# A masked-adjacency kernel: engine order remade for the loads' landing marks, a second bank for the counts, finer last loads, and two late drains on VectorE

## The chip, the cores and the metric

One core of a Trainium2 chip runs the kernel. The metric is the device time of one execution in microseconds (us). Before the change it is 188.82 us, the median of three runs (188.42 to 188.97).

## What is computed

```python
h = relu(layernorm(x))                    # x: 4096 x 64, fp32
support = h @ weight                      # 64 x 64
mask = adj != 0                           # adj: 4096 x 4096, fp32 (64 MB)
rank = cumsum(mask, axis=1); deg = rank[:, -1:]
k = minimum(deg, 100); pos = rank - (deg - k)
w = mask * where(pos > 0, 0.5 ** (k - pos), 0)
out = x + w @ support + bias
```

Each row of the adjacency keeps its last 100 neighbours and weights them by powers of one half, counted from the row's end. The output is small. The 64 MB of `adj` have to come in once.

## The kernel before

Rows are taken in 32 **tiles** of 128 rows. One tile is 2 MB of `adj` and takes this way:

- SyncE issues `load` (line 295) into one of NA = 4 buffers `a_sb`. Tiles 0, 1 and 28 to 31 come as two loads of four column groups, the others as one load of eight.
- VectorE runs `convert` (L496: nonzero test to bytes), one instruction for each load, and `flip` (L506: 32x32 block transposes into `mt`).
- TensorE runs `totals` (L512, 8 matmuls into a PSUM tile of pool `ps_t`). ScalarE runs `split` (L517), TensorE `suffix` (L526, 9 matmuls, again in `ps_t`), and VectorE `clamp` (L530). These count, for each block, the neighbours to its right.
- TensorE runs `place` (L538 and L542, 8 and 16 matmuls) into four PSUM tiles of pool `ps_v`, one for each j. ScalarE runs `weigh` (L551, Exp) four times, one j each, into a weight buffer `wk`.
- For each pair of tiles, TensorE runs `aggregate` (L559): 8 steps of 4 matmuls with `hr`, which holds `support` in two parts, into the PSUM tile `acc`.
- For each four tiles, `drain` (L572, ScalarE) takes `acc` out and adds the bias, `turn_back` (L580, TensorE) transposes back, `finish` (L586, VectorE) adds `x`, and a store follows. The last four tiles are drained in two halves.

Ahead of this stands a **prologue**: TensorE turns and centres `x`, ScalarE squares and rectifies it, VectorE takes the root, `scale` (L472) forms `support`, and `first` (L479, ScalarE) and `second` (L482, VectorE) write `hr`. The intermediate tensors lie in `early`, which is one of the NW = 2 weight buffers. Two weight buffers are all there are, so the `weigh` of tile 2 can start only when the four `second` no longer need `early`. GpSimd builds constants, among them the matrices `near`, `rest` and `far` of `order_of` (L375 to L389).

**What sets the order.** `tasks()` lists every step with its engine, an assumed duration, what it needs, and the pool that it takes a buffer from. `plan()` walks through it like a scheduler: on each engine it takes the step with the smallest due time from the table `DUE` among those that can start soon. The program is emitted in that order, and a dependency of each instruction on the one ahead of it on its engine keeps it there. So every engine works its list in order, and an instruction that waits holds all behind it. `plan()` assumes that a load has landed as soon as its bytes have been moved.

PSUM is given out as NV = 6 tiles of `ps_v`, NB = 1 of `ps_t`, and one `acc`. With NB = 1, `totals`, `suffix` and `turn_back` all take turns in one tile.

Of the kernel before, what the change touches and what calls it, by code (L numbers as in the profile page):

```python
# [8 lines left out]
F32 = mybir.dt.float32  # L9
# [22 lines left out]
STEP = {t: 4 for t in (0, 1, 28, 29, 30, 31)}  # L32
LOADS = [(t, h, h + STEP.get(t, 8)) for t in TILES for h in range(0, 8, STEP.get(t, 8))]

PARTLY = {31}
PARTED = (0, 1, 0, 2), (1, 2, 0, 1), (1, 2, 1, 2)
DRAINS = [(g, 0, 4, True) for g in range(7)] + [(7, 0, 2, True), (7, 2, 4, True)]
STORES = [(0, 0, 16), (1, 0, 12), (1, 12, 14), (1, 14, 16)]
NA, NM, NT, NW, NV, NB = 4, 4, 4, 2, 6, 1

DUE = {
    "fetch": [-1003, -1847],
    "load": [65, 1148, 1192, 1344, 890, 882, 1059, 807, 177, 1469, 585, 426, -306, 496, -49, 266, 921, 615, 495, 273,
    509, 817, 887, 432, 1250, 832, 1156, 645, 31, 863, 872, 512, 638, 869, 1362, 792, 926, 1009],
    "load_rest": [-481],
    "turn": [-213, 892, -361, 828, -409, -147, 168, -107],
    "turned": [-404, -273, 1152, 128, 503, 511, 433, -263],
    "center": [-857, -641, -1350, -827],
    "square": [139, -1681, -2148, -2029],
    "relu": [217, 890, -64, 143],  # L50
    "spread": [-1274, -1134, -743, -201],
    "support": [458, 166, -823, -732],
    "scale": [31, 1087, -17, 582],
    "root": [-38],
    "power": [-305],
    "constants": [-1199, 288],
    "order_of": [1110],
    "count": [174],
    "counted": [-242],
    "first": [1030, 859, 446, 134],  # L60
    "second": [869, 310, 488, 149],
    "convert": [799, 235, 213, 621, 871, 221, 1137, 339, 665, 170, 840, 839, 269, 846, 1322, 763, 1208, 992, 1053, 1092,
    755, 1566, 506, 1283, 1017, 914, 1881, 1297, 1713, 1456, 1930, 1878, 1817, 1254, 2527, 1603, 1404, 1849],
    "flip": [755, -234, 295, -127, 442, -299, 314, 236, -95, 42, 943, 437, 1189, 848, 1722, 445, 670, 663, 1043, 1071,
    1018, 1159, 1502, 907, 1558, 1730, 1512, 1723, 625, 1907, 1701, 1739, 1719, 1519, 1418, 1515, 1365, 795],
    "totals": [163, 587, 208, 187, -888, 339, 133, -152, 475, 1157, 159, 135, 674, 545, 1071, 817, 439, 1024, 1281,
    1461, 443, 2052, 963, 1181, 926, 1932, 1537, 584, 1513, 1671, 1316, 1615],
    "split": [-294, -174, -1849, -575, -454, -698, -618, -971, -742, -275, 300, 6, -214, 155, -90, -143, 509, 616, 114,
    395, 584, 524, 615, 13, 506, 320, 818, 391, 1992, 1302, 1105, 460],
    "suffix": [265, 470, 626, 553, 76, 351, -120, 701, -560, 193, 222, 311, 159, 444, 810, -221, 772, 1294, 1743, 886,  # L70
    718, 429, 591, 1159, 1296, 2185, 1511, 1501, 2001, 1496, 2127, 1546],
    "clamp": [-739, 475, 354, 317, -585, 294, 102, -276, 538, 118, 920, -398, 130, 1157, 352, 866, 900, 81, -363, 492,
    698, 1569, 702, 757, 515, 1132, 736, 1149, 1495, 1590, 1729, 1541],
    "place": [841, 96, 498, 879, 824, 837, 808, 522, 1103, 1914, 1312, 1548, 862, 1225, 743, 1302, 1785, 1644, 1994,
    1697, 1566, 1560, 1577, 1633, 2537, 1922, 1847, 2364, 2393, 2364, 1714, 1845],
    "weigh": [1655, 1181, 868, 631, 1236, 404, 1584, 1443, 897, 269, 877, 841, 328, 1501, 418, 1096, 1670, 1095, 1290,
    1045, 1295, 1247, 1314, 999, 672, 1559, 1035, 1631, 1070, 1779, 1431, 1276, 2029, 1311, 1734, 1852, 1556, 1640,
    1599, 1881, 1168, 1820, 1423, 545, 1375, 1271, 1659, 2299, 2395, 2281, 2155, 2139, 2062, 2491, 1666, 1651, 1902,
    1875, 1618, 2485, 1751, 1754, 2523, 1796, 2184, 2358, 1409, 2593, 2132, 1541, 1713, 2047, 1583, 1456, 1562, 2282,
    1641, 1846, 1727, 2021, 2924, 2344, 2590, 1925, 1978, 2498, 1946, 1761, 2622, 1817, 2190, 1884, 1953, 2032, 2057,  # L80
    2381, 2020, 2701, 1854, 2394, 2313, 2255, 1976, 2259, 1957, 2012, 1591, 2429, 2382, 2260, 2365, 3172, 2928, 2044,
    3150, 1958, 2643, 2675, 2150, 3338, 2587, 2729, 2343, 2953, 1990, 2517, 2778, 3358, 2745, 2645, 3479, 2076, 3183,
    2758, 2299, 2866],
    "aggregate": [254, 1326, 1623, 59, 522, 1349, 93, 1245, 247, 484, 1268, 1686, 2132, 1190, 2358, 448, 974, 1308,
    1356, 611, 856, 1518, 486, 1545, 1236, 918, 398, 1827, 1513, 1406, 1117, 1500, 1296, 1193, 452, 1811, 1260, 1164,
    1961, 1568, 1038, 1010, 1127, 1422, 1532, 1050, 1941, 1756, 685, 1493, 1977, 1124, 1719, 1240, 1199, 787, 2328,
    1076, 2631, 1964, 1500, 1168, 989, 1906, 1959, 931, 1528, 1194, 1746, 1676, 1766, 1637, 1602, 1588, 2104, 1990,
    1832, 1942, 1495, 1697, 1592, 2020, 1907, 2085, 1379, 1230, 1622, 2213, 2061, 2515, 2853, 1453, 2287, 1736, 1377,
    1679, 1972, 1745, 1669, 2617, 3235, 2571, 1770, 2567, 1656, 2752, 2666, 1678, 2311, 2453, 2712, 2395, 2976, 2826,
    2628, 2119, 2143, 2488, 2511, 1602, 2160, 1962, 2594, 2032, 2291, 2585, 1920, 2821],  # L90
    "drain": [82, 374, 29, 620, 400, 1392, 1843, 1544, 1599],
    "turn_back": [572, 1129, 645, 1544, 2558, 1512, 1987, 1280, 2435],
    "finish": [79, 927, -547, 514, 1225, 592, 1061, 2342, 2532],
    "store": [8458, 8834, 7981, 9977],
}
WAIT = 250, 60, 150, 60, 0
PE, DVE, ACT, POOL, SP = range(5)


def tasks():  # L100
# [12 lines left out]
    for n, (t, _, _) in enumerate(LOADS):  # L113
        task("load", (n,), SP, n, 0, 0, [("convert", m) for m in range(n) if LOADS[m][0] == t - NA])
    task("load_rest", (), SP, 4, 0, 0, [("load", 2)])
    for h in range(2):
        for t0 in range(0, 16, 4):
            task("turn", (h, t0), PE, 0, 430, 680, [("fetch", h)], ("v", ("turned", h, t0)))
            task("turned", (h, t0), ACT, 0, 480, 640, [("turn", h, t0)])
    for n in range(4):  # L120
        task("center", (n,), PE, 1, 860, 1060, [("turned", 1, 12)], ("v", ("relu", n)))
        task("square", (n,), ACT, 1, 480, 640, [("center", n)])
        task("relu", (n,), ACT, 2, 480, 640, [("square", n)])
    for n in range(4):
        task("spread", (n,), PE, 2, 850, 1050, [("square", n)])
    for n in range(4):
        task("support", (n,), PE, 15, 890, 1090, [("relu", n), ("power",)], ("v", ("scale", n)))
        task("scale", (n,), DVE, 10, 610, 730, [("support", n), ("power",)])
    task("root", (), DVE, 3, 480, 600, [("spread", 3)])
    task("power", (), DVE, 3, 1950, 2010, [("root",)])  # L130
    task("constants", (0,), DVE, 0, 530, 620, [])
    task("constants", (1,), POOL, 6, 4500, 4600, [("constants", 0)])
    task("order_of", (), POOL, 1, 3500, 3600, [("constants", 0)])
    task("count", (), PE, 14, 180, 360, [("order_of",)], ("v", ("counted",)))
    task("counted", (), DVE, 14, 160, 250, [("count",)])
    for i in (0, 2, 1, 3):
        task("first", (i,), ACT, 15, 520, 650, [("scale", i % 2 * 2 + 1), ("support", 3)])
        task("second", (i,), DVE, 15, 610, 740, [("first", i)])
    for n, (t, k0, k1) in enumerate(LOADS):
        k = k1 - k0  # L140
        task("convert", (n,), DVE, when[t], 311 * k + 20, 311 * k + 190, [("load", n)], ("b", ("flip", n)))
        task("flip", (n,), DVE, when[t] + 2, 136 * k + 66, 136 * k + 186, [("convert", n)] + ([("place", t - NT)] if t >= NT else []))
    for t in TILES:
        due = when[t] + 3
        parts = range(len(PARTED)) if t in PARTLY else (0,)
        task("totals", (t,), PE, due, 330, 550, [("flip", n) for n, load in enumerate(LOADS) if load[0] == t], ("t", ("split", t)))
        task("split", (t,), ACT, due + 0.5, 476, 616, [("totals", t)] + ([("suffix", t - 2)] if t > 1 else []))
        task("suffix", (t,), PE, due + 1, 618, 838, [("split", t)], ("t", ("clamp", t)))
        task("clamp", (t,), DVE, due + 1.5, 391, 511, [("suffix", t), ("counted",)] + ([("place", t - 2)] if t > 1 else []))
        task("place", (t,), PE, due + 2, 700, 920, [("clamp", t), ("constants", 1)], ("v", *[("weigh", t, j, parts[-1]) for j in range(4)]))  # L150
        for part in parts:
            a0, a1, s0, s1 = PARTED[part] if t in PARTLY else (0, 2, 0, 2)
            hold = (a1 - a0) * (s1 - s0) * 213 + 52
# [3 lines left out]
    for u in range(16):  # L157
        t = 2 * u + 1
        for k in range(8):
# [3 lines left out]
            if k == u % 2 == 0 and u:  # L163
                needs.append(("drain", u // 2 - 1))
# [470 lines left out]
```

## Time and profile before

| | us |
|---|---|
| median of 3 runs | 188.82 |
| profiled execution | 188.37 |
| its span, first to last instruction | 186.7 |
| TensorE busy (2080 matmuls) | 164.9 |
| ScalarE busy | 152.1 |
| VectorE busy | 146.8 |
| GpSimd busy | 18.9 |
| DMA queue of the loads, share of 16 engines' span | 88.4% |

The page has, for each engine, busy time in 40 slices of 4.67 us; a chain of the work that ended last; and groups of equal instructions with their mean duration, the idle time ahead of them and what ended it. The timeline view lists instructions in order of time. Of each load the trace also records when each of its 16 parts landed; the last of these is called the load's **last mark** here. For tile 2 it comes at 22.1 us, for tile 3 at 27.0, then about every 4.9 us: tile 26 at 141.48, tile 27 at 146.39, the halves of tiles 28 to 31 at 148.92, 151.38, 153.87, 156.36, 158.85, 161.34, 163.83 and 166.32. Of the last load the first part landed at 162.88. In the text, tile numbers stand in brackets: `weigh`(30, 2) is j = 2 of tile 30, `aggregate`(14, 4) is step 4 of the pair of tiles 28 and 29.

### The profile page before, as it was taken

To read this page: it belongs to the slowest core of one execution; us is meant where nothing else is said; L and a number is where in the kernel's file an instruction comes from. 1 tells how busy PE (TensorE), PEld (TensorE's weight loads), DVE (VectorE), ACT (ScalarE), POOL (GpSimd) and SP (SyncE) were. 2 spreads that over 40 slices of the span, in tenths; PEclk is the share of its full clock that TensorE was granted. 3 is DMA by queue.
4 is the path that set the end of the run, shared out by engine and by line. 5 is a ranking of instruction groups with operands and counts; after the bars stand their busy time and mean duration, and the time that the engine had idled before them with its cause. 6 is when DMAs were issued, how large, how long until landed. Compare 5 with 4: busy or idle time off the path is not lost.

```text
span 186.7 us, 4747 instructions
## 1 busy us (share of the span) xinstructions
PE 164.9 (88%) x2080; PEld 127.3 (68%) x2080; DVE 146.8 (79%) x152; ACT 152.1 (82%) x198; POOL 18.9 (10%) x57
## 2 busy tenths in 40 slices
PE   7999699647989899889998997999898979897982
PEld 5957367435857768667676775877775858685881
DVE  3187499999999997799797899879798989993100
ACT  2773176912999999699999999999969799999951
POOL 7899500000000000000000000000000000000000
PEclk9997569999999999999999999999999999999999
DMA  6999999999999999999999999999999999940020
GB/s 202 390 427 435 435 420 425 416 428 428 428 414 428 434 414 432 428 414 442 411 428 428 418 432 421 418 446 411 428 421 414 413 420 416 417 201 0 12 90 16
DMA packets 6597, 69.55 MB, mean 373 GB/s; under 512 B 944, under 2 KB 1200, under 8 KB 1712
## 3 DMA queue, kind: packets, MB, share of 16 engines
q1 hardware_dynamic: 6416, 69.21, 88.4%
q8 instruction: 16, 0.26, 0.6%
q10 hardware_dynamic: 160, 0.03, 0.1%
q14 instruction: 5, 0.04, 0.1%
HBM read 68.19 MB, written 1.05 MB: 371 GB/s over the span
## 4 chain that ended last, share of the span: by engine, by line
ACT 36%; PE 32%; DVE 15%; POOL 10%; issue 5%; POOLq 0%; ACTq 0%
ACT wk L551 29%; PE acc L559 19%; DVE m L496 7%; ACT sums L517 5%; PE ps L526 5%; PE po L580 3%; DVE mt L506 3%; PE v L542 2%; DVE behind L530 2%; PE v L538 2%; PE tot L512 2%; ACT acc_sb L572 1%; DVE wk L472 1%; DVE hr L482 1%; POOL where L414 1%
## 5 line engine op out<-in xcount | busy, mean ns | idle before, releaser
L551 ACT ACTIVATE wk<-v 128x1024 fp32r<-128x1024 uint8 (+2 forms) x136 | 123.2, 1028 | 2.3 <-PE v L542 2.1
L496 DVE TENSOR_SCALAR m<-a_sb 128x4096 uint8<-128x4096 f32 (+1 forms) x38 | 84.8, 2238 | 5.0 <-DMA a_sb<-in_adj_dram 5.0
L559 PE MATMUL acc<-wk,hr 128*128 128x256 f32 x512 | 74.6, 291 | 3.7 <-ACT wk L551 2.2
L559 PEld LDWEIGHTS acc<-wk,hr 128*128 128x128 f32 x512 | 64.0, 188 | 10.6 <-ACT wk L551 4.3
L506 DVE STREAM_TRANSPOSE mt<-m 128x1024 f32<-128x1024 f32 (+1 forms) x38 | 40.7, 1072 | 0.4
L517 ACT ACTIVATE sums<-tot 128x512 f16<-128x512 uint8 x32 | 20.3, 634 | 16.4 <-PE tot L512 16.4
L530 DVE TENSOR_SCALAR behind<-ps,excess 128x256 f16<-128x256 f32 x32 | 15.4, 481 | 14.1 <-PE ps L526 13.9
L526 PEld LDWEIGHTS <-far 128*128 128x128 f16 x224 | 17.9, 101 | 1.9 <-POOL far L389 1.0
L526 PE MATMUL ps<-sums,far 128*128 128x224 f16 (+6 forms) x224 | 18.5, 225 | 0.7 <-POOL far L389 0.7
L512 PE MATMUL tot<-mt,band 128*32 128x256 f16 x256 | 13.5, 288 | 5.3 <-DVE mt L506 4.3
L538 PE MATMUL v<-behind,where 32*128 32x256 f16 x256 | 13.6, 276 | 2.7 <-DVE behind L530 2.3
L542 PE MATMUL v<-mt,tri 32*32 32x512 f16 x512 | 14.5, 401 | 0.0
L586 DVE TENSOR_TENSOR xr<-po,xr 128x256 f32<-128x256 f32 (+1 forms) x9 | 3.5, 393 | 12.4 <-PE po L580 12.3
L423 PE MATMUL none<-junk 128*128 128x256 bf16 x74 | 11.9, 318 | 1.1 <-DVE junk L307 1.1
L512 PEld LDWEIGHTS <-band 128*32 128x32 f16 x256 | 4.1, 95 | 11.3 <-DVE mt L506 6.1
L423 PEld LDWEIGHTS <-junk 128*128 128x128 bf16 x87 | 8.8, 109 | 3.8 <-DVE junk L307 1.1
L526 PE MATMUL ps<-sums,near 128*128 128x256 f16 x32 | 9.2, 286 | 2.0 <-ACT sums L517 1.8
L572 ACT ACTIVATE acc_sb<-acc,bias_sb 128x512 f32<-128x512 f32 (+1 forms) x9 | 6.1, 679 | 5.4 <-PE acc L559 5.4
L580 PE MATMUL po<-both,acc_sb 128*128 128x64 f32 x64 | 8.7, 275 | 1.9 <-DVE behind L530 1.3
L580 PEld LDWEIGHTS po<-both,acc_sb 128*128 128x128 f32 x64 | 7.8, 191 | 2.8 <-DVE behind L530 1.5
L538 PEld LDWEIGHTS <-where 32*128 32x128 f16 x256 | 4.5, 92 | 7.5 <-issue 4.7
L542 PEld LDWEIGHTS <-tri 32*32 32x32 f16 x512 | 4.4, 88 | 6.9 <-issue 6.9
(86 smaller groups left out, 91.0 us busy)
## 6 DMA issues: line engine op xcount, KB each, us to landing
a_sb<-in_adj_dram SPq DMA_DIRECT2D x26, 2048.0 KB, 15.3
a_sb<-in_adj_dram SPq DMA_DIRECT2D x12, 1024.0 KB, 13.2
xr<-in_x_dram SPq DMA_DIRECT2D x2, 512.0 KB, 3.9
out_dram<-xr SPq DMA_DIRECT2D x1, 512.0 KB, 17.1
out_dram<-xr SPq DMA_DIRECT2D x1, 384.0 KB, 2.3
out_dram<-xr SPq DMA_DIRECT2D x2, 64.0 KB, 1.6
w<-in_L_gnn_weight_dram ACTq DMA_DIRECT2D x2, 16.0 KB, 5.8
bias_sb<-in_L_gnn_bias_dram SPq DMA_DIRECT2D x1, 0.2 KB, 18.8
```

Of the source, the lines that this page charges most:

```text
L423: nc.tensor.matmul(idle[0][:, idle[1]:idle[1] + 2 * P], junk[:, :P], junk, start=not accs, stop=not accs, skip_group_check=True)
L496: nc.vector.tensor_scalar(words[n][:, :(k1 - k0) * P, :].rearrange("p (h q) e -> p h e q", q=P), tiles[t][:, k0 * W:k1 * W].rearrange("p ( ...
L506: nc.vector.transpose(to[:, k0:k1], m_v.rearrange("p (h c l) -> p h c l", c=4, l=SUB))
L512: nc.tensor.matmul(tot[SUB * c:SUB * (c + 1), :V], band[:, SUB - 12 - 4 * a:2 * SUB - 12 - 4 * a], masks[t][:, c, :, a], start=(a == 0), s ...
L517: nc.scalar.activation(sums8[t], pts.pop((t, "n"))[:, :V].bitcast(U8).rearrange("p (i f) -> p f i", f=4)[:, :2, :], AF.Copy, bias=-136.0)
L526: nc.tensor.matmul(o, l, m, start=(k == 0), stop=(k == len(todo) - 1), skip_group_check=True)
L530: nc.vector.tensor_scalar(behind[t], pts.pop((t, "s"))[:, :V], excess, float(MAX_NEIGH), op0=ALU.subtract, op1=ALU.min)
L538: nc.tensor.matmul(vs[t, j][:, a, :], where[q, a, :], behind[t][q, :], start=(a == 0), stop=False, skip_group_check=True)
L542: nc.tensor.matmul(vs[t, j][SUB * c:SUB * (c + 1), :, :], tri[q, q], masks[t][q, c, :, :].rearrange("p i a -> p a i"), start=False, stop=T ...
L551: nc.scalar.activation(wts[u][:, s0:s1, 8 * a0:8 * a1, i, j, :], v[:, s0:s1, 8 * a0:8 * a1], AF.Exp, scale=-LN2, bias=-38.0 * LN2)
L559: nc.tensor.matmul(accs[g][:, at:at + 2 * P], hr[:, h * 4 + 2 * a + s, :, :].rearrange("p s d -> p (s d)"), wts[u][:, s, 8 * a + h].rearra ...
L580: nc.tensor.matmul(pts["o", d][:, k, :], sums[d][:, k * P:(k + 1) * P], both, start=True, stop=True)
```

## The change

- **Landing marks.** `plan()` adds `late` to the landing of a load: 0.85, 1.75 or 3.2 us, growing with the time. The table `DUE` is new throughout, so that all five lists are in a new order. FREE, the times from which the engines are assumed free, is new too.
- **Steps.** `convert` of a whole tile is now two instructions of four groups each. `aggregate` now runs over the column groups h, with 4 matmuls for one group. The layout of `ps_v` and `wk` follows this, so that the `weigh` of tile 31 is cut by groups (0 to 3, 4 and 5, 6 and 7).
- **Banks.** NB = 2, NV = 5.
- **Last loads.** Tiles 30 and 31 come as loads of four, two and two groups.
- **Drains.** `drain`(6), of tiles 24 to 27, and `drain`(7), of tiles 28 and 29, run on VectorE.
- **Prologue.** `order_of` moves from GpSimd to VectorE and the remaining constants on GpSimd get smaller; `xt`, `sq` and `rx` get parts of `early` of their own; the bias load is cut into rows 0 to 7 and 8 to 63.

The new orders, where the prediction needs them (C convert, F flip, CL clamp, DR drain, FIN finish, W weigh, PL place, TOT totals, SUF suffix, SP split, AG aggregate, TB turn_back; letters are pieces of a tile):

```
VectorE, early: C0a F0a C0b F0b C1a F1a C1b root F1b power scale0-2 C2a C2b second0 F2 CL0 scale3 second2 CL1 second1 C3a second3 C3b C4a C4b F3 CL2 F4
VectorE, late:  C27a C27b CL26 F27 C28a C28b FIN5 F28a F28b CL27 C29a C29b CL28 F29a F29b C30a C30b F30a C30c F30b F30c CL29 C31a C31b F31a CL30 C31c DR6 F31b F31c FIN6 CL31 DR7 FIN7 FIN8
ScalarE, late:  SP30 W(29,0-3) W(30,0) SP31 W(30,1-3) W(31,0-3, first part) W(31, 8 pieces) DR8
TensorE, late:  TOT30 PL29 AG(13,5) SUF30 AG(13,6-7) PL30 TB6 TOT31 AG(14,0-1) SUF31 AG(14,2-3) PL31 AG(14,4-7) AG(15,0) TB7 AG(15,1-7) TB8
before, VectorE early: C2 scale0 F2 CL1 scale1-2 C3 CL2 F3 scale3 second0 second2 C4 CL3 F4 C5 CL4 F5 second1 second3 C6
before, TensorE late:  PL30 TOT31 AG(14,0-2) SUF31 AG(14,3-4) PL31 TB6 AG(14,5-7) AG(15,0) TB7 AG(15,1-7) TB8
```

```diff
-STEP = {t: 4 for t in (0, 1, 28, 29, 30, 31)}
-PARTED = (0, 1, 0, 2), (1, 2, 0, 1), (1, 2, 1, 2)
-DRAINS = [(g, 0, 4, True) for g in range(7)] + [(7, 0, 2, True), (7, 2, 4, True)]
-NA, NM, NT, NW, NV, NB = 4, 4, 4, 2, 6, 1
+CUTS = {0: ((0, 4), (4, 8)), 1: ((0, 4), (4, 8)), 28: ((0, 4), (4, 8)), 29: ((0, 4), (4, 8)), 30: ((0, 4), (4, 6), (6, 8)), 31: ((0, 4), (4, 6), (6, 8))}
+PARTS = {31: ((0, 4), (4, 6), (6, 8))}
+DRAINS = [(g, 0, 4, g < 6) for g in range(7)] + [(7, 0, 2, False), (7, 2, 4, True)]
+NA, NM, NT, NW, NV, NB = 4, 4, 4, 2, 5, 2
...
+def late(at):
+    return 850 if at < 17000 else 1750 if at < 104000 else 3200
...
             landed = at + lag
+            lag += late(landed)
...
-        nc.sync.dma_start(bias_sb[:D], bias.rearrange("(d o) -> d o", o=1))
+        b = bias.rearrange("(d o) -> d o", o=1)
+        for d0, d1 in ((0, 8), (8, D)):
+            nc.sync.dma_start(bias_sb[d0:d1], b[d0:d1])
...
     def order_of():
-        vec = nc.gpsimd
+        vec = nc.vector
...
-    def convert(n):
+    def convert(n, i):
...
+        k0, k1 = 4 * i, min(4 * i + 4, h1 - h0)
...
-                nc.tensor.matmul(vs[t, j][SUB * c:SUB * (c + 1), :, :], tri[q, q],
-                                 masks[t][q, c, :, :].rearrange("p i a -> p a i"), start=False, stop=True, skip_group_check=True)
+                nc.tensor.matmul(vs[n, j][SUB * c:SUB * (c + 1), h0:h1], tri[q, q],
+                                 masks[t][q, c, r, :].rearrange("p (h r) a -> p h a r", r=SUB), start=False, stop=True, skip_group_check=True)
...
-    def aggregate(u, k):
+    def aggregate(u, h):
...
-        for h in range(k % 2 * 4, k % 2 * 4 + 4):
-            nc.tensor.matmul(accs[g][:, at:at + 2 * P], hr[:, h * 4 + 2 * a + s, :, :].rearrange("p s d -> p (s d)"),
-                             wts[u][:, s, 8 * a + h].rearrange("p i j r -> p (i j r)"), start=(k == h == 0),
+        for e in range(4):
+            a, s = e // 2, e % 2
+            nc.tensor.matmul(accs[g][:, at:at + 2 * P], hr[:, h * 4 + e, :, :].rearrange("p s d -> p (s d)"),
+                             wts[u][:, s, 2 * h + a].rearrange("p i j r -> p (i j r)"), start=(h == order[0] and e == 0),
```

## The prediction, made before the changed kernel had run

> **What bounds the kernel now.** I read the slices of the page first, then its chain, the waits, and the timeline around the places that these name.
>
> ```profile
> DVE  3187499999999997799797899879798989993100
> ACT  2773176912999999699999999999969799999951
> ...
> DMA  6999999999999999999999999999999999940020
> ...
> ACT 36%; PE 32%; DVE 15%; POOL 10%; issue 5%; POOLq 0%; ACTq 0%
> ```
>
> The DMA engines are full from the second slice to the 35th, and the last load's last mark is at 166.32. Yet the chain runs through ScalarE and TensorE, and ScalarE is full to the 38th slice (177 us). So the loads set a floor, and ScalarE ends late behind it. Why late? ScalarE is nearly empty in slices 4, 5, 9 and 10; the timeline of the last two (37 to 47 us) says what it waited for: counts of tiles whose turn for W had not come.
>
> ```profile
> 39.23 0.46 DVE L530 TENSOR_SCALAR behind<-ps,excess 128x256 f16<-128x256 f32 x1
> ...
> 41.42 0.60 ACT L517 ACTIVATE sums<-tot 128x512 f16<-128x512 uint8 x1 [4.00 <-PE tot L512]
> ...
> 44.79 1.26 DVE L482 TENSOR_TENSOR hr<-wk,hr 128x512 fp32r<-128x512 f32 x2
> ...
> 45.46 0.60 ACT L517 ACTIVATE sums<-tot 128x512 f16<-128x512 uint8 x1 [3.44 <-PE tot L512]
> ...
> 46.09 7.44 ACT L551 ACTIVATE wk<-v 128x1024 fp32r<-128x1024 uint8 x8
> ```
>
> W(2,0) starts at 46.09, when the last `second` (L482) has let go of `early`. From there ScalarE has hardly a gap (64.2 of 66 us busy in the window 46 to 112). One tile costs it four W at 0.92 start to start (8 in 7.44), a SP at 0.60, and a quarter of a DR at 0.57: 4.42. The loads bring a tile every 4.9. From 46.09 it gains 0.48 a tile on them, too little: W(31,0) should come at 46.09 + 29 x 4.42 = 174.3. The end of it:
>
> ```profile
> 166.71 0.71 DVE L506 STREAM_TRANSPOSE mt<-m 128x512 f32<-128x512 f32 x1
> ...
> 168.99 0.70 DVE L506 STREAM_TRANSPOSE mt<-m 128x512 f32<-128x512 f32 x1
> ...
> 171.98 5.02 ACT L551 ACTIVATE wk<-v 128x1024 fp32r<-128x1024 uint8 x7
> ...
> 177.46 0.47 ACT L572 ACTIVATE acc_sb<-acc,bias_sb 128x256 f32<-128x256 f32 x1 [0.46 <-PE acc L559]
> 177.83 2.31 ACT L551 ACTIVATE wk<-v 128x256 fp32r<-128x256 uint8 x8
> 177.98 0.53 PEld L559 LDWEIGHTS acc<-wk,hr 128*128 128x128 f32 x4 [0.83 <-ACT acc_sb L572]
> ...
> 178.89 3.38 PEld L559 LDWEIGHTS acc<-wk,hr 128*128 128x128 f32 x28
> ...
> 182.58 0.47 ACT L572 ACTIVATE acc_sb<-acc,bias_sb 128x256 f32<-128x256 f32 x1 [2.44 <-PE acc L559]
> ```
>
> The last flip ends at 169.69, W(31,0) starts at 174.8 (three W of 0.92 after 171.98), near that sum. AG(15,0) waits for DR7, then TensorE needs 4.5 us for AG(15) and TB7, and DR8 starts at 182.58. The span ends 4.1 later, at 186.65.
>
> [...] the first load's last mark is at 9.00 and its convert starts at 9.03. [...] AG(15,0), in other columns of `acc` than DR7 reads, waits for it (0.83 above). [...] By mean durations two half converts cost 2 x 1375 - 2637 = 113 ns more than a whole one. Start to start two take 2.52 against 2.55, because they overlap. I take nothing.
>
> **The change, part by part.**
>
> *Prologue.* `order_of` costs GpSimd 8.0 us (13.58 to 21.6). On VectorE it is 13 instructions: six small ones at about 0.16 (L393 to L396: 144 to 172 ns) and seven of 128 columns at about 0.25 (L349, 64 columns: 248), together 2.7. VectorE has waited up to 9.03 for the first load. The constants end at about 2.0, so this and `stack` (0.74) end at about 5.5: cost nothing; were the load early, 2.7.
>
> *The new early order on VectorE.* From C1b at 16.53 I add start to start: C 1.26, root 0.75, F1b 0.64, power 2.0, three scale at 0.62: 23.1, past tile 2's mark (22.10). C2 2.55, second 0.6, F2 1.16, CL0 0.4, scale 0.62, second 0.62, CL1 0.4, second 0.62, C3a 1.26, second 0.62: the last `second` ends at 31.9 instead of 46.05. Then C3b, C4 and F3 (5.0) bring CL2 to 36.9, PL2 ends at 38.7, and W(2,0) starts at about 38.75. ScalarE gets there in time: W(0,0) at 28.8, seven more W, `first` and two SP end at 38.1. It is a **head start of 7.3 us**. At 4.42 a tile it is worth keeping only until the loads are reached: tile k can start W no sooner than 3.9 after the mark of tile k+1 (CL26 stands behind C27: 146.44 + 2.53, then clamp 0.48 and place 0.8). 38.75 + 4.42 (k - 2) meets this at tile 18 (109.5 against 105.71 + 3.9). From there the loads and VectorE bound the kernel, with ScalarE waiting.
>
> *The end.* VectorE works without a gap from C29b (156.41). Costs: C of four groups 1.26, of two 0.65 (estimate: half, plus overhead), F 0.63 and 0.36 to 0.44, CL 0.39. Sum up to CL29: 7.2, so 163.6; C31a waits for its mark, 163.88. Then C31a 1.26, C31b 0.65, F31a 0.63, CL30 0.39, C31c 0.64 (mark 166.32, start 166.8), DR6 0.60, F31b 0.36, F31c 0.44: **168.85**. DR6 is new here. The nearest row is L472, 672 ns from PSUM with 512 columns; bounds 0.55 to 0.75. It delays the last flips by all of it, and takes 0.57 from ScalarE, where it would have stood in a wait. Smaller last loads let C31a and C31b be done before 166.32: without them C of four groups would start at 166.4, +0.6.
>
> ScalarE meanwhile: CL29 ends 163.7, PL29 164.5, W(29) 164.55 to 168.25, PL30 (needs W(29,2), 167.35) 168.2, W(30,0) to 169.2. TensorE: TB6 (8 matmuls, 0.92) 168.2 to 169.1, TOT31 0.4, SP31 0.6: 170.15. W(30,1-3): 172.9. AG(14,0-1) ends 170.35, SUF31 0.65, CL31 0.5: 171.6. PL31 waits for W(30,2), 172.0, with 0.85: 172.85. W(31) first parts 4 x 0.54: 175.1. AG(14,4-7), 16 matmuls at 0.118: 174.7. DR7 on VectorE, 0.43 to 0.5 (L530, 256 columns from PSUM: 481): 175.2; behind it VectorE has only FIN7 and FIN8. AG(15,0) 0.47, TB7 0.45, 28 matmuls 3.3, their tail 0.15: 179.65. DR8 at 179.75, and 4.1 as before: **span 183.85**, 2.8 less. ScalarE's last W ends at 177.4, so TensorE ends last.
>
> *Banks.* With NV = 5, PL(t+1) finds one tile free and its j = 3 waits for W(t,2), not W(t,1). From there to its end I take 0.85 (five matmuls of L538 and the 16 of L542: 0.20 + 0.44, with 0.2 of waits); the cover is W(t,3), 0.92, or 1.5 where a SP stands between. Cost nothing up to 0.3 a tile. NB = 2 lets TOT start without CL of the tile before: no gain where ScalarE is full, up to 0.5 at the end.
>
> *DMA.* Loads of two groups: a load of four takes 2.49 against half of 4.905, so 0.04 for each load more; two more, 0.08. The bias: one more issue, by SyncE, with loads queued: nothing; 0 to 0.3. The loads issue when `convert` has freed a buffer, with two or more queued (15 us from issue to landing), so marks stay.
>
> **Sum.** Span 183.85 and the 1.67 around it give 185.5 for an execution like the profiled one (188.37). The median lies 0.45 above that: 188.82 - 2.8 = **186.0**.
>
> **The rivals.**
>
> 1. *Slower: the missing sixth bank.* PL(t+1) comes too late for ScalarE in each tile, and TensorE, which stands still in it, is late with the rest. To give back the 7.3 us and 1 more, ScalarE has to lose 0.29 a tile: 38.75 + 29 x 4.73 = 175.9 for W(31,0) against 174.8. Then 189.9. Against it: in tiles 9 to 16 a SP mostly stands between W(t,2) and W(t+1,0), and TensorE needs 3.8 of 4.4 us. For it: ScalarE has no spare time up to tile 18. 11%.
> 2. *Part of it is lost in the tail.* Marks 1 to 2 us later than in this trace (parts of one load land up to 3.4 apart), or TB6 and AG(14) in the way: 187.5 to 188.6. 17%.
> 3. *Faster.* If AG(14) were through before PL31, TensorE would follow ScalarE: 177.4 + 1.1, DR8 at 178.6: 184.85. 12%.
>
> **How the numbers follow.** Forecast 60%, own range 185.2 to 186.9. Range 184.4 to 188.5: it takes in rival 3 and most of 2. Faster by over 0.3% (about what a measurement tells from none) is the forecast, rival 3 and two thirds of rival 2: 0.83; same 0.06; slower 0.11.
>
> **What would show it.** W(2,0) near 39, all `second` done by 33; gaps ahead of L570's SP or W after about 110 us; last flip near 168.9; DR8 near 179.8. If ScalarE shows no gap up to 170 us, rival 1 or its mild form holds. If the last mark isn't near 166.3, the end moves with it.

## The result and the profile after

Twelve executions of each kernel give 187.36 us after (186.39 to 188.47) and 188.69 before (188.17 to 189.1): ratio 0.9927, 95% interval 0.9909 to 0.9945. Beside the experiments after was measured again: 186.95, ratio 0.9908 (0.9874 to 0.9942). The change makes the kernel faster, by 1.3 to 1.7 us; 2.8 were forecast. Of the executions below, one each of E1, E2 and E3 and two each of E7 and E9 lay over 1.5% above the fastest of their kernel; ratios leave these out, medians don't.

The profiled execution of after is the slowest of its twelve: 188.47 us, span 186.5. First its slices, then its chain by engine:

```profile
DVE  6288799999989898899998889988897989996110
ACT  2664046999999979879999999799949899999951
PEclk9998599999999999999999999999789999999999
DMA  6999998999999999999999999999999999950200
...
DMA 36%; PE 31%; DVE 16%; ACT 13%; issue 2%
```

The chain has changed sides: before it had ScalarE 36% and no DMA; now it has DMA 36% and ScalarE 13%. ScalarE has dips at slices 15, 18 and 26, where it was full before, and its deepest one behind the prologue at slice 30 (4 tenths; 6 before). And TensorE's clock has a dip at slices 29 and 30 (133 to 137 us); before had such dips only in the prologue. The timeline of after at the places that were shown of before (start, duration, engine, line, operation, idle time ahead and what ended it):

```profile
32.13 0.68 DVE L525 TENSOR_TENSOR hr<-wk,hr 128x512 fp32r<-128x512 f32 x1
...
39.02 3.77 ACT L617 ACTIVATE wk<-v 128x1024 fp32r<-128x1024 uint8 x4
...
138.33 1.03 ACT L617 ACTIVATE wk<-v 128x1024 fp32r<-128x1024 uint8 x1 [2.41 <-PE v L603]
...
168.99 0.75 DVE L652 TENSOR_SCALAR acc_sb<-acc,bias_sb 128x512 f32<-128x512 f32 x1
169.66 0.76 DVE L554 STREAM_TRANSPOSE mt<-m 128x256 f32<-128x256 f32 x2
...
174.42 0.40 PE L599 MATMUL v<-behind,where 32*128 32x256 f16 x8
...
177.88 0.70 PE L637 MATMUL acc<-wk,hr 128*128 128x256 f32 x4 [0.67 <-DVE acc_part L652]
...
178.78 3.54 PE L637 MATMUL acc<-wk,hr 128*128 128x256 f32 x28
...
182.36 0.47 ACT L650 ACTIVATE acc_part<-acc,bias_sb 128x256 f32<-128x256 f32 x1 [2.79 <-PE acc L637]
```

The head start is there: the last `second` ends at 32.8 (46.05 before), and W(2,0) starts at 39.02 (46.09). Yet DR8 starts at 182.36, against 182.58 before: in this execution the 7 us are all gone. The wait of 2.41 us ahead of W(23,0) says where some went. The windows view cuts this stretch along TensorE's clock; the columns are busy time (and instructions) of TensorE, its weight loads, VectorE, ScalarE and GpSimd, then the granted clock, the DMA share and GB/s:

```profile
126.31:129.73 3.42, 3.42 (x51) 2.56 (x48) 2.71 (x3) 3.42 (x5) 0.00 (x0) 1.00 1.01 427
129.73:133.14 3.41, 2.07 (x42) 1.35 (x41) 2.74 (x4) 3.41 (x6) 0.00 (x0) 1.00 0.99 423
133.14:136.55 3.41, 3.41 (x21) 3.15 (x21) 3.01 (x4) 2.79 (x4) 0.00 (x0) 0.50 1.02 432
136.55:139.97 3.42, 3.42 (x50) 2.48 (x50) 3.42 (x4) 1.64 (x3) 0.00 (x0) 1.00 1.00 422
```

From 133.14 to 136.55 TensorE runs at half its clock and gets through 21 instructions in place of some 50. In the 3.41 us ahead of it, it had been busy for only 2.07. PL23 comes late, and ScalarE loses 1.8 of the next 3.4 us.

### The profile page after: what moved, and what is told of

It is laid out like the page before. It is cut to its first block, busy times and chain, and to the rows that moved or that the text cites. A ratio compares the mean times of both kernels' runs of the same rounds, so it can differ in the third digit from the quotient of the medians.

```text
span 186.5 us, 4785 instructions
## 1 busy us (share of the span) xinstructions
PE 167.0 (90%) x2083; PEld 131.2 (70%) x2083; DVE 151.8 (81%) x197; ACT 152.9 (82%) x196; POOL 6.8 (4%) x43
## 3 DMA queue, kind: packets, MB, share of 16 engines
HBM read 68.19 MB, written 1.05 MB: 371 GB/s over the span
## 4 chain that ended last, share of the span: by engine, by line
DMA 36%; PE 31%; DVE 16%; ACT 13%; issue 2%
DMA a_sb<-in_adj_dram 36%; PE acc L637 11%; DVE m L544 11%; ACT wk L617 10%; PE pp L512 3%; PE sums L583 2%; PE sums L658 2%; PE none L494 2%; PE v L603 2%; PE pc L482 2%; PE none L467 2%; PE v L599 2%; ACT wk L478 2%; DVE hr L525 1%; ACT sums L570 1%
## 5 line engine op out<-in xcount | busy, mean ns | idle before, releaser
L544 DVE TENSOR_SCALAR m<-a_sb 128x2048 uint8<-128x2048 f32 (+1 forms) x66 | 86.4, 1359 | 10.9 <-DMA a_sb<-in_adj_dram 10.9
L554 DVE STREAM_TRANSPOSE mt<-m 128x1024 f32<-128x1024 f32 (+2 forms) x40 | 40.8, 1029 | 0.4
L570 ACT ACTIVATE sums<-sums 128x512 f16<-128x512 uint8 x32 | 19.9, 626 | 11.1 <-PE sums L562 10.5
L589 DVE TENSOR_SCALAR behind<-sums,excess 128x256 f16<-128x256 f32 x32 | 15.2, 477 | 5.7 <-PE sums L583 5.7
L583 PE MATMUL sums<-sums,far 128*128 128x224 f16 (+6 forms) x224 | 18.1, 222 | 0.0
L562 PE MATMUL sums<-mt,band 128*32 128x256 f16 x256 | 13.0, 281 | 1.7 <-DVE mt L554 1.6
L467 PE MATMUL none<-junk 128*128 128x256 bf16 x70 | 10.1, 306 | 1.2 <-DVE junk L353 1.2
L583 PE MATMUL sums<-sums,near 128*128 128x256 f16 x32 | 9.1, 284 | 2.4 <-ACT sums L570 2.2
L583 PE MATMUL sums<-sums,rest 128*128 128x256 f16 x32 | 8.8, 277 | 0.0
L658 PE MATMUL sums<-both,acc_sb 128*128 128x64 f32 x56 | 7.6, 279 | 0.6 <-ACT acc_sb L650 0.6
L658 PEld LDWEIGHTS sums<-both,acc_sb 128*128 128x128 f32 x56 | 6.8, 191 | 1.4 <-ACT acc_sb L650 0.7
```

The lines of the kernel that those rows point to most:

```text
L467: nc.tensor.matmul(idle[0][:, idle[1]:idle[1] + 2 * P], junk[:, :P], junk, start=not accs, stop=not accs, skip_group_check=True)
L544: nc.vector.tensor_scalar(words[n][:, k0 * P:k1 * P, :].rearrange("p (h q) e -> p h e q", q=P), tiles[t][:, (h0 + k0) * W:(h0 + k1) * W].r ...
L554: nc.vector.transpose(to[:, h0:h1], m_v.rearrange("p (h c l) -> p h c l", c=4, l=SUB))
L562: nc.tensor.matmul(tot[SUB * c:SUB * (c + 1), r], band[:, SUB - 12 - 4 * a:2 * SUB - 12 - 4 * a], masks[t][:, c, r, a], start=(a == 0), st ...
L570: nc.scalar.activation(sums8[t][:, :, r], pts.pop((n, "n")).bitcast(U8).rearrange("p (i f) -> p f i", f=4)[:, :2, r], AF.Copy, bias=-136.0)
L583: nc.tensor.matmul(o, l, m, start=(k == 0), stop=(k == len(todo) - 1), skip_group_check=True)
```

## The experiments

The theories, as the expectations name them. **A**: from about tile 10 on the loads' last marks set the pace; what is missing went to half-speed windows of TensorE, late marks and the tail. **B** (the prediction's first rival): the missing sixth bank. **C**: the second bias load delays the marks. **D**: the head start alone is not enough, the order behind it is needed. **E**: fillers don't govern the windows. **F**: a bank is missed only by an order made for six. **G**: the head start isn't needed, VectorE's clamps set the end in any case.

One table for all, from the profiled execution of each (us). "Half speed" are the windows after 26 us:

| kernel | half speed at | last mark | W(2,0) | W(31,0) | DR8 | span | median, ratio to before |
|---|---|---|---|---|---|---|---|
| before | none | 166.32 | 46.09 | 174.94 | 182.58 | 186.7 | 188.69 |
| after | 133.1 | 167.04 | 39.02 | 175.28 | 182.36 | 186.5 | 187.36, 0.9927 |
| E1 after again | 28.2, 55.5 (two) | 166.58 | 37.10 | 173.49 | 180.63 | 184.8 | 186.95, 0.9908 |
| E2 one filler more | 169.6 | 166.67 | 38.80 | 175.09 | 182.24 | 186.4 | 187.66, 0.9945 |
| E3 bias in one | 28.1, 55.4 (two) | 166.45 | 37.45 | 173.38 | 180.52 | 184.6 | 187.62, 0.9932 |
| E4 drains on ScalarE | 132.1 | 166.24 | 38.82 | 174.91 | 181.96 | 186.1 | 187.51, 0.9929 |
| E7 45 fillers more | none | 165.89 | 38.00 | 173.25 | 180.40 | 184.5 | 187.64, 0.9938 |
| E8 W in quarters | 77.1 (two) | 167.06 | 38.67 | 175.95 | 183.03 | 187.2 | 187.16, 0.9925 |
| E11 no filler behind 40 us | 56.1, 121.0 | 166.22 | 37.12 | 173.71 | 180.85 | 185.0 | 187.82, 0.9950 |
| E9 order, late start | 34.0 | 167.10 | 49.51 | 177.15 | 184.30 | 188.4 | 189.32, 1.0023 |
| E5 head start alone | none | 168.45 | 40.71 | 175.49 | 183.14 | 187.2 | 190.90, 1.0109 |
| E6 five banks alone | 85.8 | 170.81 | 46.60 | 184.87 | 192.52 | 196.6 | 198.75, 1.0533 |
| E10 both bank counts alone | 44.2, 122.7, 163.7 | 166.46 | 47.30 | 186.46 | 193.26 | 197.3 | 198.14, 1.0509 |
| E12 VectorE 2.5 later | 131.8, 159.2 | 166.37 | 38.78 | 177.14 | 184.22 | 188.3 | 190.79, 1.0111 |

**E1: after, profiled again.** No edit.

> The changed kernel once more, for a second profile. Theory A (the loads' last marks set the pace from about tile 10 on, and the missing 1.4 us of the forecast went to TensorE windows at half speed, late marks and the tail): the time is 187.0 to 187.6 us, and where the profile shows no half-speed window after 30 us, CL26, W(30,0) and DR8 come 0.5 to 1.5 us earlier than in the first profile of after (150.67, about 170.6, 182.36), while the gaps of ScalarE before W stay. Theory B (the missing sixth bank holds ScalarE up in every tile, clock or not): the same gaps and the same lateness without any half-speed window, DR8 again near 182.4.

Measured: 186.95 us; no half-speed window after 63 us, and CL26 at 149.21 (150.67 in the first profile), W(30,0) at 168.50 (170.49), DR8 at 180.63 (182.36). The last two are earlier by more than the 1.5 us that were expected. The gaps of ScalarE stay (W after `place`: 4.2 us in 7). That is theory A's form and not B's. It also gives the execution that the prediction should be held against. Its end on TensorE and VectorE:

```profile
167.65 0.75 DVE L652 TENSOR_SCALAR acc_sb<-acc,bias_sb 128x512 f32<-128x512 f32 x1
...
168.30 0.77 DVE L554 STREAM_TRANSPOSE mt<-m 128x256 f32<-128x256 f32 x2
...
171.50 1.19 PE L637 MATMUL acc<-wk,hr 128*128 128x256 f32 x8
171.69 0.48 DVE L589 TENSOR_SCALAR behind<-sums,excess 128x256 f16<-128x256 f32 x1 [1.68 <-PE sums L583]
172.62 0.40 PE L599 MATMUL v<-behind,where 32*128 32x256 f16 x8
...
176.15 0.71 PE L637 MATMUL acc<-wk,hr 128*128 128x256 f32 x4 [0.67 <-DVE acc_part L652]
...
180.63 0.47 ACT L650 ACTIVATE acc_part<-acc,bias_sb 128x256 f32<-128x256 f32 x1 [2.86 <-PE acc L637]
```

**E2, E7, E11: TensorE's fillers.** Fillers are matmuls on a tile of zeros that the kernel issues where `plan()` sees TensorE idle. E2 puts back the thresholds of before, which the change had raised, E7 raises a cap, and E11 takes all fillers away after 40 us:

```diff
-... "place": 1024, ... "turn_back": 2048
+... "place": 800, ... "turn_back": 512
```
```diff
-            idle = max(0, min(int((at - end) * 0.6) // 110, (4200 - recent) // 256))
+            idle = max(0, min(int((at - end) * 0.6) // 110, (9000 - recent) // 256))
```
```diff
-            idle = max(0, min(int((at - end) * 0.6) // 110, (4200 - recent) // 256))
+            idle = max(0, min(int((at - end) * 0.6) // 110, (4200 - recent) // 256)) if at < 40000 else 0
```

> After with the thresholds for TensorE's filler matmuls that before had (place 800, turn_back 512): only a few fillers more, order unchanged. Theory A: if TensorE falls to half speed because it is fed less, the mean clock rises by about 0.005 to 0.009 (half to one window of 3.41 us) and the time falls by 0.4 to 0.8 us against after, to about 186.7. Theory B, and a theory that the windows fall in covered work: no difference, within 0.2 us. If the fillers themselves stand in the chain: slower by up to 0.5 us.

> After with the cap on TensorE's filler matmuls in 3.4 us raised from 4200 to 9000 rows: 80 fillers of 256 columns more after 40 us, in stretches where the order leaves TensorE idle; all else in place. Theory A (half-speed windows late in the run cost 1.7 us each, and they come where TensorE stood idle in the window ahead): hardly a window after 120 us, the spread of the runs shrinks, median 186.5 to 186.9 us. Rival E (windows don't depend on how TensorE is fed that finely, or the fillers stand in the chain): spread and median as after, 187.2 us or more.

> After without any filler matmul planned later than 40 us (45 fewer, which stood at 55 to 75, 120, 130 and 150 to 160 us). If TensorE's half-speed windows come where it stood idle in the window ahead: more windows after 50 us, mean clock lower by 0.01 or more, 0.5 to 2 us more than after. If the windows don't depend on fillers: as after, 187.2 to 187.6 us, clock 0.97 to 0.98.

Measured: the edits did less than the expectations say. Those count planned fillers: behind 40 us 45 in after, 52 in E2, 125 in E7, none in E11. But the kernel leaves out the ones that fall between a `drain` and the next `aggregate`: the traces have 20, 21, 65 and 0. So E2 is after with a single filler more. The mean clock over each kernel's executions is 0.970 in E11, 0.974 in after and in E2, 0.981 in E7. The times don't follow (187.82, 187.36 and 186.95, 187.66, 187.64); all intervals overlap. Theory A's expectations failed here: E7's median isn't lower, its executions spread over 2.5 us (after: 2.1), and E11's clock is lower by 0.003 and not by 0.01. E7 suggests that fillers raise the clock, but E4 (0.979) and E9 (0.981) come as high without these edits, so theory E is neither shown nor refuted. As an edit, fillers are worth nothing that shows.

The profiles say more on the windows. The eight from after to E11 in the table have nearly the same order, and they fall into two groups: DR8 at 180.40 to 180.85 where no window comes after 125 us and no pair at 77, and at 181.96 to 183.03 where one does. A window behind 125 us goes with 1.1 to 2.0 us. The groups were formed after the fact; within one execution, E2 shows it. In the tail it runs as E1 does (W(30,0) at 168.23 and 168.50) up to its window at 169.55; then the same matmuls take longer. First E1, then E2:

```profile
169.48 0.41 PE L562 MATMUL sums<-mt,band 128*32 128x256 f16 x8
...
169.82 1.21 PE L637 MATMUL acc<-wk,hr 128*128 128x256 f32 x8
...
170.87 0.28 PE L583 MATMUL sums<-sums,near 128*128 128x256 f16 x1
```
```profile
169.57 0.62 PE L562 MATMUL sums<-mt,band 128*32 128x256 f16 x8
...
170.12 2.08 PE L637 MATMUL acc<-wk,hr 128*128 128x256 f32 x8
...
172.00 0.44 PE L583 MATMUL sums<-sums,near 128*128 128x256 f16 x1
```

TOT31 starts 0.09 behind E1, SUF31 1.13, and DR8 1.61: this late window cost about 1.5 us.

**E3: the bias load in one piece.**

```diff
-        for d0, d1 in ((0, 8), (8, D)):
+        for d0, d1 in ((0, D),):
```

> After with the bias load in one piece of 64 rows again. Theory C (the extra bias DMA makes one of the 16 parts of the queued loads late, the +1.0 us that the marks jump between tiles 4 and 5): marks from tile 5 on come 0.7 to 1.0 us earlier (tile 27 near 146.4, the last near 166.3), time 0.4 to 0.8 us less than after. Theory A without C: marks as in after within 0.3 us on the average, time within 0.2 us of after.

Measured: the last mark is at 166.45. In the seven others of that group, with the split, it lies at 165.89 to 167.06. The jump of the marks between tiles 4 and 5 is still there (31.68 to 37.33), and it is in E5 and E6 too, which have one bias load. Theory C falls; the 0.7 us by which the first profile of after was later than before is within what one execution differs from another.

**E4: drains 6 and 7 back on ScalarE.**

```diff
-DRAINS = [(g, 0, 4, g < 6) for g in range(7)] + [(7, 0, 2, False), (7, 2, 4, True)]
+DRAINS = [(g, 0, 4, True) for g in range(7)] + [(7, 0, 2, True), (7, 2, 4, True)]
```

> After with drain(6) and drain(7) back on ScalarE. By the prediction's own terms drain(6) on VectorE costs the last flips all of its 0.75 us, and ScalarE has waits to take it: the last flip 0.7 us earlier, but drain(7) then stands among the W of tile 31 and aggregate(15,0) waits for it: time 0.3 to 0.7 us less than after. Rival (the drains on VectorE are what the tail gains from): 0.5 to 1.0 us more than after, with TensorE's wait ahead of aggregate(15,0) grown by that.

Measured: 187.51, as after. Neither gain nor loss can be shown; the intervals can't tell less than about 0.5 us. In the profile both halves of the expectation are there: from the start of the last `convert` to that of the last flips it takes 0.64 us in place of 1.37, and TensorE's wait for drain 7 is 0.96 in place of 0.67.

**E8: finer W of tile 31.**

```diff
-PARTS = {31: ((0, 4), (4, 6), (6, 8))}
+PARTS = {31: ((0, 2), (2, 4), (4, 6), (6, 8))}
```

> After with the W of tile 31 cut into pieces of two groups from the start (16 pieces, not 4 of four groups and 8 of two). The tail's theory: TensorE ends last, and aggregate(15,0) waits for PL31 and for W(31) of all four j over groups 0 to 3; with pieces of two it could start about 1 us earlier, if drain(7) allows. If W(31) bounds that start: 0.4 to 0.8 us less than after. If TensorE itself with AG(14) and drain(7) bounds it: no difference, or 0.3 us more[...].

The edit also adds four due times for the four more steps. Measured: 187.16, as after. In its profile AG(15,0) now runs straight behind AG(14), ahead of drain 7, and the next AG waits 0.58 for drain 7 instead; from the start of PL31's last 16 matmuls (175.41) to DR8 it takes 7.62 us, in E1 (172.95 to 180.63) 7.68. TensorE and drain 7 bound this stretch, not W. In after a W of two groups starts 0.264 us behind the one ahead of it, a W of four groups 0.478; by these four more W cost ScalarE 0.2 us in all.

**E5 and E9: the head start without the order, and the order with a late start.** E5 is before, E9 is after, each with one edit, from which `plan()` makes the order anew:

```diff
-    "second": [869, 310, 488, 149],
+    "second": [-9000, -9000, -9000, -9000],
```
```diff
-    "second": [-75, 111, -482, -354],
+    "second": [6500, 6600, 6700, 6800],
```

> The kernel before with one edit: due times of the four second of -9000, so that they run on VectorE ahead of clamp(3); nothing else of the change. All second end near 36, W(2,0) starts near 37.5 instead of 46.09. Theory A (the head start is what the change gains, and with it the loads and TensorE bind the end): 186.7 to 187.7 us, with W(14,0) some 3 us earlier than before, ScalarE in gaps after it, and runs that spread as those of after do (over 2 us, against 0.9 of before). Rival D (the new order behind the head start, made for the last marks, is needed too): over 188.2 us, the lead gone at the end.

> After without the head start: due times of the four second raised to 6500 to 6800, so that the last of them stands behind flip of tile 6 on VectorE and W(2,0) starts near 47.5, later than in before; VectorE's order from tile 17 on is unchanged. The prediction's own sum (ScalarE at 4.42 a tile from there): W(31,0) at 47.5 + 29 x 4.42 = 175.7 and a time of 189.5 us or more. New theory G (the end is set by VectorE's clamps behind the loads, which W has caught up with by about tile 22 in any case; what the change gains is that VectorE is no longer late there): CL26 near 149.2, W(31,0) near 173.5 where no half-speed window comes late, time 186.8 to 187.8 us, as after.

Measured: E5 is slower than before, 190.90, and E9 no faster, 189.32 (1.0001 to 1.0044). ScalarE in E9:

```profile
49.51 1.03 ACT L617 ACTIVATE wk<-v 128x1024 fp32r<-128x1024 uint8 x1 [4.09 <-DVE hr L525]
...
174.19 7.24 ACT L617 ACTIVATE wk<-v 128x1024 fp32r<-128x1024 uint8 x15
```

Theory G falls: VectorE's clamps don't set the end whatever the start. The prediction's sum for ScalarE holds: from W(2,0) at 49.51, 29 tiles of 4.42 give 177.7 for W(31,0); it starts at 177.15 (the fourth of the 15), 4.40 a tile. So ScalarE does bound the order of after when it starts late enough, and this start cost 189.32 - 187.36 = 2.0 us against after.

That is not the worth of the forecast's head start. W(2,0) of E9 is 10.5 us later than in the first profile of after, and also 3.4 later than in before, so E9 is not the new order with before's start. An estimate for that one, from E9's own rate: 46.09 + 29 x 4.40 = 173.7 for W(31,0) (the rate is from one execution, 1.1 us above E9's median), where E1 has 173.49 and before 174.94. By this estimate the new order has most of its gain without any head start over before. It was not run, so what the head start itself is worth stays open.

In E5 the lead of W(2,0) is 5.4 us, of W(10,0) 2.0, of W(18,0) 0.9, and W(22,0) is 0.5 late. ScalarE's timeline shows two of the waits in which it went:

```profile
65.20 3.77 ACT L551 ACTIVATE wk<-v 128x1024 fp32r<-128x1024 uint8 x4 [1.60 <-PE v L542]
...
74.30 0.60 ACT L517 ACTIVATE sums<-tot 128x512 f16<-128x512 uint8 x1 [0.68 <-PE tot L512]
```

The order that `plan()` makes from before's due times lost the early start: theory D. But E5's loads also came late: its last mark is at 168.45, 2.1 us behind that of before, and W(31,0) follows it by 7.0 us, as in E1 (6.9). What the order lost and what the late loads lost was not separated. E5's median is higher still than its profile (span 187.2, clock 0.977); its five other executions had a clock of 0.946 to 0.953, by an estimate from the clocks (1.7 us lost to a window) five or six half-speed windows against two or three.

**E6 and E10: the banks by themselves.** Both are before. E6 leaves its order as it is; in E10 the planner knows of both numbers:

```diff
-    ps_v = ctx.enter_context(tc.tile_pool(name="ps_v", bufs=NV, space=bass.MemoryType.PSUM))
+    ps_v = ctx.enter_context(tc.tile_pool(name="ps_v", bufs=5, space=bass.MemoryType.PSUM))
```
```diff
-NA, NM, NT, NW, NV, NB = 4, 4, 4, 2, 6, 1
+NA, NM, NT, NW, NV, NB = 4, 4, 4, 2, 5, 2
```

> The kernel before with five tiles in ps_v instead of six, order unchanged. Before is held by ScalarE from 46 us on, so a missing bank shows at once. Prediction's step: up to 0.3 us a tile of cover, cost nothing: 188.4 to 189.0 us, W at 0.92 start to start still. Rival 1: 0.29 us or more a tile, 25 tiles, time 192 us or more. Between (190 us): some tiles lose their cover.

> The kernel before with the banks of after alone: five tiles in ps_v, two in ps_t, both known to the planner, which makes its order for them from the old due times. Taking one tile away under the old order cost 10.1 us. Theory F (the order had PL wait for a tile that was no longer there, with all of TensorE's list behind it; an order that knows of five doesn't): 188.0 to 190.0 us. Rival 1 (five tiles cost ScalarE 0.3 to 0.5 us a tile however they are planned): 194 us or more.

Measured: 10.1 and 9.5 us more. Both expectations of "nothing" failed, and F with them. Of TensorE's waits between 46 and 160 us (total, times, longest), the line of `place` behind W, first in before, then in E6, then in E1:

```profile
PE v L538 <- ACT wk L551: 0.4, 2, 0.2
```
```profile
PE v L538 <- ACT wk L551: 6.4, 13, 1.1
```
```profile
PE v L599 <- ACT wk L617: 1.7, 3, 0.7
```

With five tiles, PL(t+1) has to wait for W(t,2), and all that stands behind it on TensorE waits too. After has five tiles as well and waits 1.7 us where E6 waits 6.4. So rival 1's mechanism is real in E6, which loses 0.35 us a tile. It isn't only that after has slack where it waits for loads: E9, with the same five tiles and ScalarE full, keeps 4.40 a tile. So the rest of the change keeps the cost off. Which of its moves does so wasn't tried: one due table makes all five lists, and the change also has four buffers in place of two for what `clamp` writes. In E10 this wait is only 2.7 us in all; where the rest of its 9.5 us goes stays open.

**E12: VectorE 2.5 us later at 151 us.** The `convert` of the first half of tile 28 is done three times:

```diff
-        nc.vector.tensor_scalar(words[n][:, k0 * P:k1 * P, :] ...
+        for _ in range(3 if n == 30 else 1):
+            nc.vector.tensor_scalar(words[n][:, k0 * P:k1 * P, :] ...
```

> After with the convert of the first half of tile 28 done three times in place of once (the same bytes written again), 2.5 us more for VectorE near 151 us; nothing else. The prediction's end, and theory G (from about 150 us VectorE works without a gap behind the loads and sets the end): the last flip 2.1 to 2.5 us later, DR8 with it, 2 us more than after, 189.2 to 189.8 us. If TensorE or ScalarE bounds the tail by themselves: under 0.7 us more.

Measured: 190.79, 3.4 more than after, where 2 were expected. VectorE's timeline, with the `convert` of tile 28 (four instructions now) and the two last flips:

```profile
151.31 5.50 DVE L545 TENSOR_SCALAR m<-a_sb 128x2048 uint8<-128x2048 f32 x4
...
171.51 0.76 DVE L555 STREAM_TRANSPOSE mt<-m 128x256 f32<-128x256 f32 x2
```

The last flips start 1.85 us later than in the first profile of after (169.66), which also had a half-speed window near 133, and DR8 is 1.86 later; 2.1 to 2.5 were expected. The end follows VectorE, and the rival (under 0.7 us) falls. That the median moved by more than 2.5 isn't explained by this. A second window at 159.2 in this profile, behind a stretch in which TensorE was busy for 1.2 of 3.4 us, suggests that the added wait also starves TensorE.

Not tried one by one: the finer last loads, NB = 2, the planner's landing marks, and `order_of` on VectorE.

## Why the prediction was right, and where its sum failed

The direction was right, and so was the bound that the kernel moves to: the loads. The gain was half as large, and that it comes from the head start wasn't shown (E9). The sum was a span of 183.85, 1.67 around it, and 0.45 from the profiled execution to the median. An execution without a late window (E1) has a span of 184.75 and 2.01 around it, and the median of after lies 0.60 above it. The three differences, 0.90, 0.34 and 0.15, are the 1.4 us that are missing.

- **What bounds before.** ScalarE at 4.42 a tile from 46.09: E9 confirms the rate to 0.6 us in 128. It was not the whole: in E5 the start is 5.4 us earlier and the end no better.
- **Prologue, head start.** W(2,0) forecast at 38.75, measured 37.1 to 39.02; `order_of` ends at 5.3, ahead of the first load's last mark at 9.53. Right, with some luck: "PL2 ends at 38.7" is 0.5 over the sum of its own terms (36.9 + 0.48 + 0.8), and CL2 came 0.7 later than forecast (37.64 in the first profile of after).
- **Where the loads are reached.** Forecast: tile 18, by "CL stands behind the next tile's C", which I had read at CL26. In the early order CL8 and CL10 stand behind C of the tile after the next, so ScalarE's gaps begin at 65.7 (E7) to 67.0 us (after). From W(10,0) to W(18,0) (75.45 and 111.52 in E7) it takes 4.5 a tile, and it meets the loads for good at tile 22: last mark of tile 23 at 127.09 in E1 plus 3.9 is 131.0, and W(22,0) starts at 131.45. From 46 to 112 us the loads move 427 GB/s in after and 425 in before, with a DMA share of 1.01 in both. The place was wrong; for the end it made no difference.
- **The end on VectorE.** End of the last flip forecast for 168.85 with the last mark at 166.32; E1 169.07 with 166.58, E7 168.40 with 165.89. Right, though DR6 took 0.75 and not 0.60. E12 shows that the end follows VectorE.
- **The step that failed: TensorE's walk through the tail, from "PL30 ... 168.2" to "AG(15,0)".** In E1 TB6 waits for DR6, which ends at 168.40 (0.23 from the later marks, 0.15 from DR6's length), and TB6 and TOT31 take longer than reckoned. SP31 ends at 170.6, not 170.15, so that W(30,2) ends at 170.50 + 2 x 0.92 = 172.34, not 172.0. And "PL31 waits for W(30,2)" left out AG(14,2-3), which stands ahead of it in the order shown: it holds PL31 to 172.62. PL31 ends at 173.40, 0.55 late. AG(14,4-7) takes 2.15 where 16 x 0.118 = 1.9 was reckoned; drain 7, with its waits, 0.67 and not 0.5. AG(15,0) is thus 0.95 late (176.15 against 175.2), and the rest took 4.48 in place of 4.55: DR8's 0.88. No one term is large: 0.34, 0.21, 0.23 and 0.17.
- **"1.67 around it".** It was taken from the rounded span 186.7; with 186.65, which the same sum uses, it is 1.72. Every kernel from after has 1.98 to 2.02 us outside the span, every one from before 1.71 to 1.74, whatever the edit. What of the change adds this 0.3 stays open: none of the experiments undid it.
- **The half-speed windows** were not in the prediction, not even as a rival. That the 0.45 which I added to reach the median was near the 0.60 measured was luck: in after the distance holds late windows, of which the sum knew nothing. They go with the spread of after's executions, 2.1 us (before: 0.9), and 6 of 17 executions fall in rival 2's range, 187.5 to 188.6.
- **Banks.** "Cost nothing up to 0.3 a tile" came true by luck, not by the reason given: the same reasoning fits before's order, where it costs 10 us. A chance of 11% was too low for what the argument could bear.

Why do the windows hurt after and not before? Before's 80 executions at a clock of 0.968 and above have a mean of 188.66, its 10 at 0.962, by the same estimate one window more, 188.61: no cost. After's have 186.88 at 0.98 (6), 187.47 at 0.97 (8), 188.02 at 0.963 (2): some 0.6 us for a window. In E7 and E9 the same comparison gives about 0.9, in E3 nothing, so windows are a part of the spread and not all of it. Two reasons are suggested by the traces, not shown. Before's windows in its profile lie at 16 to 26 us, ahead of ScalarE's own long wait. And between 48 and 175 us, the stretches of 3.41 us in which TensorE is busy for less than 2.4 have their starts within 2.3 us in all in before, within 10.6 and 4.8 us in the two profiles of after: TensorE is fed less evenly where loads set the pace.

## What to carry to other kernels

When a head start moves the bound to another engine, check that the order behind it can use it: here the head start alone was 1.1% slower, and the whole change 0.7 to 0.9% faster. To price the head start, take it back to where it was and not further: E9 went 3.4 us past it, and the question stayed open. Count what ran and not what was planned: of 80 planned fillers, 45 ran. In a tail, walk each engine's list with every entry that stands ahead and with start-to-start times: here terms of 0.17 to 0.34 us, all in TensorE's walk and all of one sign, added up to a third of the forecast gain. And when the bound goes from an evenly working engine to transfers, look at TensorE's clock behind its waits, and price it as a spread of the result.

## What the runs showed of the hardware

**TensorE's half speed.** It comes in stretches of 3.41 us or multiples: 3.41 at 133.14 and 6.83 at 17.09 in after, 10.24 at 16.15 in before. Of the 17 stretches in the table, five with the time in which TensorE had been busy in the 3.4 us ahead: 2.07 in after (133.1), 1.67 in E1 (55.5), 2.36 in E2 (169.6), 1.94 in E4 (132.1), 1.68 in E8 (77.1). As little work stands elsewhere without such an effect: 1.80 in before (40.04 to 43.46), 2.33 in after (30.74 to 34.15). And the prologue's stretches began behind 3.4 us of work without a wait, in before and in after. So waits, of 1.05 us in all in E2, stand ahead of these five; what sets the half speed off was not shown.

**One load's parts.** In before the 16 parts of the first load land within 0.97 us (8.03 to 9.00); those of the last land within 3.44 in before (162.88 to 166.32) and 4.38 in after (162.66 to 167.04). The last mark moves by 1.2 us from one execution to another of nearly the same kernel (165.89 in E7, 167.06 in E8).
